# Layer 3 of a four-layer graph kernel: carrying a neighbour count between blocks by a row of the mask instead of by a second matrix product

## The chip, the cores and the metric

The kernel runs on one core of a Trainium2 chip. The metric is the device time of one execution in microseconds (us). Three executions of the kernel before took 552.76, 553.60 and 554.91 us; the median is 553.6 us. The profile shows one execution of the same program on the same kind of core.

The engines are named as in the profile: PE is the matrix engine (PEld its weight loads), DVE the vector engine, ACT the scalar engine, POOL the GpSimd engine, and SP an engine that here only issues DMAs.

## The reference

The input is a feature matrix x of 3327 nodes by 64 features and an adjacency matrix adj of 3327 by 3327 floats, of which a small share is not zero. Four layers follow each other; each computes x = layernorm(x + layer(x)). Layer 0 reduces to a layer norm of x. Layer 1 is a hyperbolic attention that reads all of adj. Layers 2 and 3 are the ones that matter here:

```python
# layer 2: two hops
for k in range(2):
    agg = adj @ x
    x = tanh(concat([agg, x]) @ W[k])
# layer 3
support = input @ weight
mask = (adj != 0)
rank = cumsum(mask, axis=1)
deg = rank[:, -1:]
k = minimum(deg, 100.0)
pos = rank - (deg - k)
w = mask * where(pos > 0, 0.5 ** (k - pos), 0.0)
out = w @ support + bias
```

In layer 3 the weight of a neighbour j of node i is 0.5 to the power of the number of neighbours of i that come after j, and zero from the hundredth on. So each weight needs a count over all later columns of the row.

## The kernel before, in words

The host hands over adj transposed and padded to 3328 by 3328, so rows are neighbours j and columns are nodes i. Rows are cut into NB = 26 blocks of 128, one neighbour per partition. Columns are cut into two halves (HALF = 1664), each into CPH = 4 chunks of CW = 416. One block is 1664 KB in f32, half of one 832 KB. Seven blocks stay in SBUF through layer 2 (`kept`: 25 to 22, EARLY, which stay through layer 3 too, and 19 to 21, LATE); the others are loaded by SP each time they are used, into a ring of UNDER_WAY = 4 block buffers (`strm`, tile `at_l` in the profile) and MORE = 2 further ones (`more`, tile `bt_l`).

Instructions are issued in the order in which the program writes them on PE, ACT and DVE in layers 2 and 3 (manual schedules), and SP issues the block loads in program order, each as soon as its buffer is free.

**Layer 2** (`layers`, the loop over `order`): in each hop every block is multiplied in f32. `add(c, jb)` (line 421) makes one product of 64 output rows for either half of the columns, so a block is eight products, two of them side by side in the columns of the PE array; f32 products show as two records each. The last blocks (`end`) are done chunk by chunk in `chunk_end` (the tanh is line 506), before `top` and `bottom` (lines 373, 409, 412) prepare the next hop. Blocks still in their buffers at the end of hop 1 (`ready`) are used first in hop 2. DVE and ACT have little to do.

**Layer 3** walks over 52 steps q: for each half, block 25 down to block 0. For a step

- `masks` (line 341, DVE) turns the half block into a bf16 mask of zeros and ones. It reads a kept block or a tile `ah` which SP loads just before (line 339, four buffers). It is called for step q + AHEAD = q + 3, into a ring of AHEAD + 3 = 6 mask tiles.
- `count` (line 526, PE) multiplies the mask by a 128 by 128 matrix into the PSUM tile `cnt[c]`, c = 0 or 1, of two chunks each. `tri` has 100 * 128 on its diagonal and -128 for every later row, so the result is 128 * (100 - later neighbours within the block) where there is a neighbour and something not positive elsewhere.
- `read` turns `cnt[c]` into a weight: the maximum with zero as a 16-bit integer is the bit pattern of a bf16 power of two. ACT reads c = 0 (line 541), DVE reads c = 1 (line 539).
- `products` multiplies the weights, LEAD = 3 steps later, by the support, which is split in three bf16 parts: two of them in one product of 128 rows (`high`, line 722, four per step), and the third in 64 rows (line 737), of which GROUP = 9 steps' worth, 36 products, are done in one burst.

`advance(c, q)` carries the count from block to block in PSUM: after `cnt[c]` was read for step q, `count(c, rest, q)` adds the matrix `rest`, for which tri + rest is -128 everywhere, so that `cnt[c]` then holds -128 times the neighbours seen so far; then `count(c, tri, q + 1)` adds the next block. So PE makes eight count products per step, four with `rest` and four with `tri`. In each step PE's order is: high c = 0, advance c = 0, high c = 1, (burst,) advance c = 1.

The support itself (parts `s12` and `s3`) is finished during the first steps of layer 3, by a list of small pieces of work, `with_step`, of which one is done per step; `other_parts` (line 653) is where POOL takes part. When the first half is done (`turn`), its sums are taken out and normalised beside the second half's steps (`half_out`). In layers 2 and 3 POOL does nothing else, and no DMA is issued from POOL anywhere.

Of the kernel before, what the change touches and what calls it, by code (L numbers as in the profile page):

```python
# [10 lines left out]
F32 = mybir.dt.float32  # L11
BF16 = mybir.dt.bfloat16
# [7 lines left out]
P = 128  # L20
# [21 lines left out]
UNDER_WAY = 4  # L42
MORE = 2

# [32 lines left out]
def kernel(  # L77
# [73 lines left out]
    with nc.allow_non_contiguous_dma(reason="two short columns"):  # L151
# [30 lines left out]
        pattern=[[-1, P]], channel_multiplier=1,  # L182
    )

    center = both_m[:, :P]
# [21 lines left out]
    tri = const.tile([P, P], BF16, name="tri")  # L207
    rest = const.tile([P, P], BF16, name="rest")

# [88 lines left out]
    def layer_3_constants():  # L298
        nc.gpsimd.tensor_copy(tri, tri_f)
        nc.gpsimd.tensor_scalar(rest, tri_f, -1.0, -STEP, ALU.mult, ALU.add)  # L300

        nc.gpsimd.tensor_scalar(w3_dg, w3_dg, float(2**27), None, ALU.mult)
# [9 lines left out]
    def layers(ctx, x2, x3, begun_here, kept, ready, ahead_ctx, strm):  # L312

        cols = x2.rearrange("p n d -> p (n d)")

        more_ctx = ExitStack()
        more = more_ctx.enter_context(tc.tile_pool(name="more", bufs=MORE, reuse_waits="tile"))
        l3m = None
        in_order = ctx.enter_context(ExitStack())
        in_order.enter_context(tc.manual_schedule(engines={mybir.EngineType.PE}))  # L320
        steps = [(h, jb) for h in range(2) for jb in range(NB - 1, -1, -1)]
        mask, ws = {}, {}

        def masks(q):
            nonlocal l3m
            if l3m is None:
                more_ctx.close()
                l3m = ctx.enter_context(
                    tc.tile_pool(name="l3m", bufs=AHEAD + 3, reuse_waits="tile")
                )  # L330
            if q >= len(steps):
                return
# [8 lines left out]
            nc.vector.tensor_scalar(mask[q], at, 0.0, None, ALU.not_equal)  # L341

        groups = fours
# [50 lines left out]
        )  # L394
        with tc.tile_pool(name="l2p", bufs=2, space=PSUM, reuse_waits="tile") as l2p:
            for k in range(2):
# [86 lines left out]
                for i, jb in enumerate(order):  # L483
# [6 lines left out]
                    for c in range(CPH):  # L490
                        add(c, jb)
                    if k == 0 and begun_here:

                        if i == 8:
                            for c in range(CPH):
                                bottom(c)

                            warm_t = small.tile([P, 1], F32, tag="warm", name="warm_t")
                            nc.scalar.activation(warm_t, hT[:, :1], AF.Tanh)
                    if k and jb in held and len(held) == MORE:  # L500
                        for q in range(AHEAD + 3):
                            masks(q)
# [5 lines left out]
                if k:  # L508
                    break
                for c in range(CPH):  # L510
                    chunk_end(c)
# [10 lines left out]

        def count(c, mat, q, start):
            for e in range(2):
                of = slice((2 * c + e) * CW, (2 * c + e + 1) * CW)
                nc.tensor.matmul(  # L526
                    cnt[c][:, e, :], mat, mask[q][:, of], start=start,
                    stop=(mat is tri), skip_group_check=True,
                )
# [120 lines left out]
        def other_parts(i):  # L650
            sl = slots(i)
            nc.scalar.copy(s12[:, sl, 1, :], rr[:, sl])  # L652
            nc.gpsimd.tensor_tensor(s3[:, sl], rr[:, sl], s12[:, sl, 1, :], ALU.subtract)  # L653

        with tc.tile_pool(name="l3t", bufs=2, space=PSUM, reuse_waits="tile") as l3t:
# [15 lines left out]
            first_part(A)  # L671
            count(0, tri, 0, True)
            read(0, 0, False)
# [5 lines left out]
            finish(l3t, C)  # L679
            count(1, tri, 0, True)  # L680
            squares(C)
# [32 lines left out]
        def products(q, c):  # L714
# [12 lines left out]


            later.append((q, c))
            if not last:  # L730
                high(q, c)
            if last or c and len(later) == 2 * GROUP:
# [9 lines left out]
                if last:  # L742
                    high(q, c)

        def sums_out(h):
# [63 lines left out]
        def last_out(h, accT):  # L809
# [87 lines left out]
    with tc.tile_pool(name="l1", bufs=1) as l1:  # L897
# [462 lines left out]
        def near_end(mT, ljT, xm, sq_e, t_e, rows_63, x2):  # L1360
# [4 lines left out]
            with tc.tile_pool(name="l1e", bufs=1) as l1e, tc.tile_pool(  # L1365
# [242 lines left out]
                nc.gpsimd.tensor_copy(tri, tri_f)  # L1608
                nc.gpsimd.tensor_scalar(rest, tri_f, -1.0, -STEP, ALU.mult, ALU.add)

# [266 lines left out]
```

## Time and profile before

| What | Value |
|---|---|
| Median of the three runs | 553.6 us |
| Profiled execution: its own time, and its span | 552.76 us, 552.8 us |
| Layer 2, hops 1 and 2 | about 240 to 315 and 315 to 391 us |
| Layer 3: start, steps, end | 391 to 411, 411 to 539, 539 to 553 us |
| PE busy | 524.6 us, 95% of the span |
| DVE, ACT, POOL busy | 373.2, 275.2, 207.6 us |

The profile gives, for each group of instructions with the same line and shape, the number of them, the time for which at least one was under way, and the mean duration of one. Products on PE overlap, so the spacing of their starts, not the duration of one, is what a product costs. A bracket at the end of a line of the timeline tells how long the engine sat idle before it and what released it.

### The profile page before, as it was taken

What the parts mean: (1) busy time and instruction counts of PE and PEld (TensorE: products, weight loads), DVE (VectorE), ACT (ScalarE), POOL (GpSimd) and SP (SyncE); (2) the same over time, 40 slices, a digit from 0 to 9 for tenths busy, and PEclk for the clock granted to TensorE, in tenths of its full rate; (3) what the DMA queues carried; (4) which work ended last, traced back from release to release, by engine and by line L of the source; (5) the groups of instructions that cost most, each with busy time, mean ns of one, the idle gap of its engine ahead of it and who ended that gap; (6) DMA issues with size and microseconds to landing.
All of it is one profiled execution on the core that took longest, in us unless ns stands there. A gap on an engine that the chain in (4) does not pass through costs nothing.

```text
span 552.8 us, 7387 instructions
## 1 busy us (share of the span) xinstructions
PE 524.6 (95%) x2841; PEld 228.6 (41%) x2841; DVE 373.2 (68%) x553; ACT 275.2 (50%) x321; POOL 207.6 (38%) x85
## 2 busy tenths in 40 slices
PE   8879999999999999999999999999999999989991
PEld 5622222222222222854444444444455555645551
DVE  6789999999999999899000011200679769697733
ACT  4699999999999997620000100000365333433321
POOL 3599999999999999000000000000001000000000
PEclk9799999999999999899999999999999999999996
DMA  8979667666777626699999049999019994799601
GB/s 288 341 225 301 219 224 234 212 233 208 232 240 225 209 95 277 247 427 427 421 430 395 3 167 422 429 420 383 32 53 362 323 375 140 238 295 354 244 1 37
DMA packets 33892, 143.56 MB, mean 260 GB/s; under 512 B 10269, under 2 KB 11959, under 8 KB 28855
## 3 DMA queue, kind: packets, MB, share of 16 engines
q1 hardware_dynamic: 31511, 142.40, 69.9%
q10 hardware_dynamic: 2336, 0.59, 0.5%
q8 instruction: 24, 0.39, 0.3%
q14 instruction: 21, 0.17, 0.1%
HBM read 141.53 MB, written 0.87 MB: 258 GB/s over the span
## 4 chain that ended last, share of the span: by engine, by line
PE 66%; DVE 16%; ACT 11%; issue 5%; DVEq 0%; POOL 0%; ACTq 0%; POOLq 0%
PE cnt L421 26%; PE cnt L526 11%; DVE v L1124 8%; PE pq L1103 7%; PE acc L722 6%; ACT pq L1116 5%; ACT sg L1076 5%; PE acc L1133 4%; PE acc L737 3%; DVE a L1115 2%; DVE w L539 1%; DVE mask L341 1%; PE cnt L412 1%; PE idle L928 1%; PE pm L1416 1%
## 5 line engine op out<-in xcount | busy, mean ns | idle before, releaser
L1088 POOL TENSOR_TENSOR sg<-sg,at 128x1664 f32<-128x1664 f32 x44 | 163.9, 3751 | 2.0 <-ACT sg L1076 1.9
L1103 PE MATMUL pq<-riT,ljT 64*128 64x416 f32 x416 | 100.8, 561 | 10.3 <-DVE v L1124 6.2
L1116 ACT ACTIVATE pq<-pq,al,ga 128x832 f32<-128x832 f32 x104 | 104.7, 1011 | 11.0 <-DVE a L1115 11.0
L1124 DVE SCALAR_TENSOR_TENSOR v<-pq,a 128x832 f32<-128x832 f32 x104 | 105.4, 1014 | 3.6 <-ACT pq L1116 2.5
L1115 DVE SCALAR_TENSOR_TENSOR a<-pq,sg 128x832 f32<-128x832 f32 x104 | 105.2, 1012 | 0.5 <-PE prep_fours L1194 0.5
L1133 PE MATMUL acc<-v,xv 128*64 128x416 f32 x416 | 95.3, 537 | 0.0
L1076 ACT ACTIVATE sg<-lb,rb 128x1664 f32<-128x1664 f32 (+1 forms) x53 | 87.2, 1647 | 0.0
L541 ACT ACTIVATE w<-cnt 128x832 int16<-128x832 f32 x55 | 47.2, 862 | 71.2 <-PE cnt L526 71.1
L421 PE MATMUL cnt<-at_l,lj 128*64 128x416 f32 x448 | 80.3, 513 | 0.0
L653 POOL TENSOR_TENSOR s<-sq,s 128x384 bf16<-128x384 f32 (+1 forms) x4 | 4.1, 1024 | 197.9 <-ACT s L652 197.9
L506 ACT ACTIVATE x<-cnt 128x416 f32<-128x416 f32 x8 | 4.1, 517 | 130.6 <-PE cnt L421 130.6
L1103 PEld LDWEIGHTS pq<-riT,ljT 64*128 64x128 f32 x416 | 31.3, 184 | 83.7 <-DVE v L1124 82.8
L539 DVE TENSOR_SCALAR w<-cnt 128x832 int16<-128x832 f32 x49 | 50.1, 1022 | 21.2 <-PE cnt L526 20.8
L526 PE MATMUL cnt<-mask,rest 128*128 128x416 bf16 x200 | 51.5, 339 | 2.4 <-ACT w L541 1.4
L526 PE MATMUL cnt<-mask,tri 128*128 128x416 bf16 x208 | 53.5, 339 | 0.1
L722 PE MATMUL acc<-w,s 128*128 128x416 bf16 x208 | 52.5, 339 | 0.5 <-DVE hid L794 0.5
L421 PEld LDWEIGHTS cnt<-at_l,lj 128*64 128x64 f32 x448 | 31.9, 137 | 46.1 <-issue 45.2
L1133 PEld LDWEIGHTS acc<-v,xv 128*64 128x64 f32 x416 | 20.6, 134 | 61.7 <-issue 58.0
L341 DVE TENSOR_SCALAR mask<-ah 128x1664 bf16<-128x1664 f32 x42 | 43.5, 1035 | 1.0 <-DMA ah<-in_adjT 1.0
L409 DVE COPY lj<-pn_l 128x512 f32<-128x512 f32 (+1 forms) x4 | 2.4, 592 | 60.8 <-PE pn_l L373 60.8
L421 PE MATMUL cnt<-kept,lj 128*64 128x416 f32 x224 | 41.2, 513 | 0.0
L1088 POOL TENSOR_TENSOR sg<-sg,kept 128x1664 f32<-128x1664 f32 (+1 forms) x10 | 30.0, 3026 | 0.8 <-ACT sg L1076 0.8
(291 smaller groups left out, 413.8 us busy)
## 6 DMA issues: line engine op xcount, KB each, us to landing
at_l<-in_adjT SPq DMA_DIRECT2D x24, 1664.0 KB, 12.2
at<-in_adjT SPq DMA_DIRECT2D x44, 832.0 KB, 5.0
ah<-in_adjT SPq DMA_DIRECT2D x42, 832.0 KB, 6.5
bt_l<-in_adjT SPq DMA_DIRECT2D x8, 1664.0 KB, 16.7
kept<-in_adjT SPq DMA_DIRECT2D x7, 1664.0 KB, 9.2
lb<-lf_rows SPq DMA_DIRECT2D x2, 384.0 KB, 6.3
ljT<-ljT SPq DMA_DIRECT2D x4, 128.0 KB, 2.3
x<-in_x ACTq DMA_DIRECT2D x1, 416.0 KB, 5.4
```

The costliest lines, as they stand in the source:

```text
L341: nc.vector.tensor_scalar(mask[q], at, 0.0, None, ALU.not_equal)
L421: nc.tensor.matmul(acc[c][h * D : (h + 1) * D, :], hw[:, slot(jb), :], blocks[jb][:, o : o + CW], start=c not in begun, stop=last, skip_gr ...
L526: nc.tensor.matmul(cnt[c][:, e, :], mat, mask[q][:, of], start=start, stop=(mat is tri), skip_group_check=True,)
L539: nc.vector.tensor_scalar(w.bitcast(I16), cnt[c], 0.0, None, ALU.max)
L722: nc.tensor.matmul(acc[h, c][:, e, :], s12[:, slot(jb)].rearrange("p t d -> p (t d)"), ws[q, c][:, e, :], start=first, stop=last,)
L1076: nc.scalar.activation(sg[:, :, of], lbs[:, :, of], AF.Sigmoid, bias=rb[:, sl : sl + 1])
L1088: nc.gpsimd.tensor_tensor(sg[:, :, of], sg[:, :, of], at[:, :, of], ALU.mult)
L1103: nc.tensor.matmul(pq[:, h, :], ljT[h != jb // NBH][rows, of], riT[rows, ch * CW : (ch + 1) * CW], start=True, stop=True,)
L1115: stt(a_s[t], pqs[t], CUBIC_PLUS, us.pop(t), op0=ALU.add, op1=ALU.mult)
L1116: nc.scalar.activation(pqs[t], pqs[t], AF.Square, bias=al[:, one], scale=ga[:, one])
L1124: stt(w, pqs.pop(t), CUBIC_REST, a_s.pop(t), op0=ALU.add, op1=ALU.mult)
L1133: nc.tensor.matmul(accs[cp, ci][h * D : (h + 1) * D, :], xv[:, slot(jb), :], w[:, h, :], start=(jb == orders[cp][0]), stop=(jb == orders[c ...
```

## The change

Layer 3 no longer carries the count in PSUM. The number of neighbours in all later blocks is computed beforehand, in layer 2, and handed to layer 3 in row 0 of each mask:

- In layer 2, `t_masks` makes masks of every block on DVE (two halves per block, ring of three tiles), and `t_counts` multiplies them by a 128 by 32 matrix of ones and zeros (`upto`) into two PSUM tiles `t_0`, `t_1`: four products of 32 output rows per mask, one per chunk and per quarter of the array's columns. Row r of the result is the number of neighbours in blocks r and later. Blocks from position 6 of hop 1 on are done in hop 1, the rest of the kept blocks at its end, and blocks 0 to 4 in hop 2.
- When all 26 blocks are counted, `t_out` clamps the counts at 127, writes them to DRAM (`t_rows`, four DMAs from POOL); `first_weights` loads row 0 of each block (eight DMAs from POOL) and works out the weights of the 26 first nodes.
- `masks` gets a DMA from POOL that overwrites row 0 of each of the 52 masks by the row of counts of the later blocks. Row 0 of `tri` becomes -128 throughout, so the product with `tri` subtracts them. `rest` is gone, and `count` starts a new sum for each step: four count products per step instead of eight.
- The first node of each block has lost its place in the mask; the 26 of them are an extra block of 32 rows. `first_rows` gathers their support rows into `sf` by 16 DMAs from POOL, issued with the seventh entry of `with_step` (step 9), and `first_products` adds eight products of 32 input rows per half, at block 12.
- `read` of c = 1 goes to DVE only in odd steps, and to ACT in even ones.
- MORE is 1 instead of 2, so one block buffer fewer in layer 2, and POOL too issues in program order.

```diff
-MORE = 2
+MORE = 1
+CLAMP = 127.0
+FIRST_T = 6
...
+    nc.gpsimd.memset(tri_f[:1, :], -STEP)
...
+        tmask = more_ctx.enter_context(tc.tile_pool(name="tmask", bufs=3, reuse_waits="tile"))
         more = more_ctx.enter_context(tc.tile_pool(name="more", bufs=MORE, reuse_waits="tile"))
...
             nc.vector.tensor_scalar(mask[q], at, 0.0, None, ALU.not_equal)
 
+            nc.gpsimd.dma_start(mask[q][:1, :], t_rows[jb + 1 : jb + 2, half])
...
+        def t_masks(jb):
+
+            t_done.add(jb)
+            for h in range(2):
+                m = tmask.tile([P, HALF], BF16, tag="tm", name=f"tm_{jb}_{h}")
+                nc.vector.tensor_scalar(
+                    m, blocks[jb][:, h * HALF : (h + 1) * HALF], 0.0, None, ALU.not_equal
+                )
+                t_made.append((jb, h, m))
+
+        def t_counts():
+            while t_made:
+                jb, h, m = t_made.pop(0)
+                for c in range(CPH):
+                    nc.tensor.matmul(
+                        t_ps[h][c * 32 : (c + 1) * 32, :], upto[:, 31 - jb : 63 - jb],
+                        m[:, c * CW : (c + 1) * CW], start=(h, c) not in t_begun,
+                        stop=len(t_done) == NB, skip_group_check=True,
+                    )
+                    t_begun.add((h, c))
+
+        def t_out():
+
+            for h in range(2):
+                nc.vector.tensor_scalar(tb[:, h], t_ps[h], CLAMP, None, ALU.min)
+            for c in range(CPH):
+                nc.gpsimd.dma_start(
+                    by_chunk(t_rows)[c], tb[c * 32 : c * 32 + NB + 1]
+                )
+
+        def first_weights():
+
+            firsts = by_chunk(adjT.rearrange("(b p) i -> p b i", p=P)[0])
+            for h in range(2):
+                nc.gpsimd.memset(m0, 0.0)
+                for c in range(CPH):
+                    nc.gpsimd.dma_start(m0[c * 32 : c * 32 + NB, :], firsts[c, :, h])
...
                     for c in range(CPH):
                         add(c, jb)
+                    t_counts()
+                    if jb not in t_done and (k or i >= FIRST_T):
+                        t_masks(jb)
...
-                    if k and jb in held and len(held) == MORE:
+                    if k and len(t_done) == NB and not t_made and not mask:
+                        t_out()
+                        first_weights()
                         for q in range(AHEAD + 3):
                             masks(q)
...
+                for jb in kept:
+                    if jb not in t_done:
+                        t_masks(jb)
+                        t_counts()
                 for c in range(CPH):
                     chunk_end(c)
...
-            first = steps[q + 1][1] == NB - 1
-            if not first:
-                count(c, rest, q, False)
-            count(c, tri, q + 1, first)
+            count(c, q + 1)
...
+            if c and jb == NBH - 1:
+                first_products(h)
...
+        def first_rows():
+
+            with nc.allow_non_contiguous_dma(reason="one row of each block"):
+                for cg in range(CPH):
+                    e = cg % 2
+                    for h in range(2):
+                        at = slice(cg * 32 + h * NBH, cg * 32 + (h + 1) * NBH)
+                        nc.gpsimd.dma_start(
+                            sf[at, 0, :],
+                            s12[:1, h::2].rearrange("p n t d -> p n (t d)"),
+                        )
+                        nc.gpsimd.dma_start(sf[at, 1, e * D : (e + 1) * D], s3[:1, h::2])
+
+        def first_products(h):
+
+            for part in range(2):
+                for cg in range(CPH):
+                    of = slice(cg * 32, (cg + 1) * 32)
+                    nc.tensor.matmul(
+                        acc[h, cg // 2][:, cg % 2, :], sf[of, part], tb[of, h],
+                        start=False, stop=False,
+                    )
...
-            lambda: other_parts(E), lambda: x3_later(C), lambda: x3_later(E),
+            lambda: (other_parts(E), first_rows()), lambda: x3_later(C), lambda: x3_later(E),
...
-            read(1, q, True)
+            read(1, q, q % 2 == 1)
```

More of the change, by code (lines that the diff above doesn't have):

```diff
@@ L207 @@
     tri = const.tile([P, P], BF16, name="tri")
-    rest = const.tile([P, P], BF16, name="rest")
     def block(pool, jb, **kw):
@@ L299, in layer_3_constants @@
         nc.gpsimd.tensor_copy(tri, tri_f)
-        nc.gpsimd.tensor_scalar(rest, tri_f, -1.0, -STEP, ALU.mult, ALU.add)
         nc.gpsimd.tensor_scalar(w3_dg, w3_dg, float(2**27), None, ALU.mult)
@@ L314, in layers @@
         cols = x2.rearrange("p n d -> p (n d)")
+        carry = ctx.enter_context(tc.tile_pool(name="carry", bufs=1, reuse_waits="tile"))
+        upto = carry.tile([P, 64], BF16, name="upto")
+        nc.gpsimd.memset(upto[:, :32], 1.0)
+        nc.gpsimd.memset(upto[:, 32:], 0.0)
+        tb = carry.tile([P, 2, CW], BF16, name="tb")
+        m0 = carry.tile([P, CW], F32, name="m0")
+        sf = carry.tile([P, 2, P], BF16, name="sf")
+        nc.gpsimd.memset(sf, 0.0)
+        t_rows = dram.tile([NB + 1, NP], BF16, name="t_rows")
         more_ctx = ExitStack()
+        tmask = more_ctx.enter_context(tc.tile_pool(name="tmask", bufs=3, reuse_waits="tile"))
         more = more_ctx.enter_context(tc.tile_pool(name="more", bufs=MORE, reuse_waits="tile"))
@@ L319, in layers @@
         in_order = ctx.enter_context(ExitStack())
-        in_order.enter_context(tc.manual_schedule(engines={mybir.EngineType.PE}))
+        in_order.enter_context(
+            tc.manual_schedule(engines={mybir.EngineType.PE, mybir.EngineType.Pool})
+        )
         steps = [(h, jb) for h in range(2) for jb in range(NB - 1, -1, -1)]
@@ L394, in layers, with by_chunk @@
         )
-        with tc.tile_pool(name="l2p", bufs=2, space=PSUM, reuse_waits="tile") as l2p:
+        def by_chunk(rows):
+            return rows.rearrange("b (h c k) -> c b h k", h=2, c=CPH)
+        t_done, t_made, t_begun, t_ps = set(), [], set(), []
+        def t_masks(jb):
[29 more added lines that the diff above has]
+                    nc.gpsimd.dma_start(m0[c * 32 : c * 32 + NB, :], firsts[c, :, h])
+                nc.vector.tensor_scalar(
+                    m0, m0, 0.0, (NEIGH + 1) * STEP, ALU.not_equal, ALU.mult
+                )
+                nc.vector.scalar_tensor_tensor(
+                    m0, tb[:, h], -STEP, m0, op0=ALU.mult, op1=ALU.add
+                )
+                nc.vector.tensor_scalar(tb[:, h].bitcast(I16), m0, 0.0, None, ALU.max)
+        with tc.tile_pool(
+            name="l2p", bufs=2 if begun_here else 1, space=PSUM, reuse_waits="tile"
+        ) as l2p:
+            t_ps += [
+                l2p.tile([P, 512], F32, bufs=1, tag=f"t{h}", name=f"t_{h}")[:, :CW]
+                for h in range(2)
+            ]
             for k in range(2):
@@ L515, in layers, with count @@
                 hT = nxt
-        def count(c, mat, q, start):
+        def count(c, q):
             for e in range(2):
@@ L526, in count @@
                 nc.tensor.matmul(
-                    cnt[c][:, e, :], mat, mask[q][:, of], start=start,
-                    stop=(mat is tri), skip_group_check=True,
+                    cnt[c][:, e, :], tri, mask[q][:, of], start=True, stop=True,
+                    skip_group_check=True,
                 )
@@ L671, in layers @@
             first_part(A)
-            count(0, tri, 0, True)
+            count(0, 0)
             read(0, 0, False)
@@ L679, in layers @@
             finish(l3t, C)
-            count(1, tri, 0, True)
+            count(1, 0)
             squares(C)
@@ L743, in products @@
                     high(q, c)
+        def first_rows():
[7 more added lines that the diff above has]
+                            s12[:1, h::2].rearrange("p n t d -> p n (t d)"),
+                        )
+                        nc.gpsimd.dma_start(sf[at, 1, e * D : (e + 1) * D], s3[:1, h::2])
[6 more added lines that the diff above has]
+                        start=False, stop=False,
+                    )
         def sums_out(h):
@@ L1608, in near_end @@
                 nc.gpsimd.tensor_copy(tri, tri_f)
-                nc.gpsimd.tensor_scalar(rest, tri_f, -1.0, -STEP, ALU.mult, ALU.add)
         def any_norm(m, x1):
```

## The prediction

> **What bounds the kernel now.** I read the engines' shares first, then the busy time by stage, then the chain of waits, and last the timeline of single steps.
>
> ```profile
> PE 524.6 (95%) x2841; PEld 228.6 (41%) x2841; DVE 373.2 (68%) x553; ACT 275.2 (50%) x321; POOL 207.6 (38%) x85
> ...
> 240.00:315.00 75.00, 75.00 (x423) 30.80 (x418) 21.20 (x42) 1.75 (x4) 0.00 (x0) 1.00 0.85 358
> 315.00:391.00 76.00, 76.00 (x432) 32.48 (x429) 8.75 (x11) 1.28 (x3) 0.00 (x0) 1.00 0.82 337
> ...
> 411.00:468.00 57.00, 56.70 (x354) 31.00 (x351) 48.65 (x53) 22.02 (x28) 2.07 (x2) 1.00 0.81 300
> ...
> PE cnt L421 26%; PE cnt L526 11%; DVE v L1124 8%; PE pq L1103 7%; PE acc L722 6%; ACT pq L1116 5%; ACT sg L1076 5%; PE acc L1133 4%; PE acc L737 3%; DVE a L1115 2%; DVE w L539 1%; DVE mask L341 1%; PE cnt L412 1%; PE idle L928 1%; PE pm L1416 1%
> ```
>
> The stage lines read: stage, its length, busy time of PE, PEld, DVE, ACT, POOL, then clock, DMA share and GB/s. PE is busy for all 75.00 and 76.00 us of the two hops, so whatever is added to PE there is added to the end; DVE (21.20, 8.75) is nearly free there. In layer 3's steps PE is busy for 56.70 of 57.00 us. The chain agrees: its largest pieces are the adds of layer 2 (L421) and the counts of layer 3 (L526).
>
> One step of layer 3:
>
> ```profile
> 436.63 1.02 DVE L341 TENSOR_SCALAR mask<-ah 128x1664 bf16<-128x1664 f32 x1
> 436.81 0.86 ACT L541 ACTIVATE w<-cnt 128x832 int16<-128x832 f32 x1 [1.25 <-PE cnt L526]
> 436.90 0.52 PE L526 MATMUL cnt<-mask,rest 128*128 128x416 bf16 x2
> 437.25 0.51 PE L526 MATMUL cnt<-mask,tri 128*128 128x416 bf16 x2
> 437.60 0.52 PE L722 MATMUL acc<-w,s 128*128 128x416 bf16 x2
> 437.80 1.02 DVE L539 TENSOR_SCALAR w<-cnt 128x832 int16<-128x832 f32 x1 [0.15 <-PE cnt L526]
> ...
> 438.92 0.86 ACT L541 ACTIVATE w<-cnt 128x832 int16<-128x832 f32 x1 [1.25 <-PE cnt L526]
> ...
> 449.65 3.36 PE L737 MATMUL acc<-w,s 128*64 128x416 bf16 x36
> 452.94 0.52 PE L526 MATMUL cnt<-mask,rest 128*128 128x416 bf16 x2
> ```
>
> A step is 438.92 - 436.81 = 2.11 us: twelve products starting 0.176 us apart. Each ninth step has the burst: 36 products, two abreast, in 3.29 us (0.091 each), with the switch 3.38. Nine steps: 9 x 2.11 + 3.38 = 22.4 us, 2.49 a step; ACT waits 1.25 us per step for PE.
>
> **Part 1, narrow products in layer 2: +18.5.** 52 masks, four products each, 416 columns. Four abreast a mask costs one start, 0.176. If only two run abreast as in the burst, 4 x 0.091 = 0.364; one after the other, 4 x 0.176 = 0.70. The burst is nearest (also a part of the array's columns, own weight load each) and shows overlap; four quarters should overlap further, so I take the middle of the first two, 0.27: 14.0. The program's order has 22 separate groups of them between the f32 adds; two changes of product shape cost 0.2 (the burst takes 3.38 where 18 x 0.176 = 3.17 would do): 4.4. Sum 18.5; ends 13.6 and 41. It all lies on the path.
>
> **Part 2, masks of layer 2 on DVE: +4.7.** 104 halves at 1.02 (L341) would be 106; there are 52, 53 us, beside 151 us of PE with 30 us of DVE, so they are hidden, except at the end of hop 1. There, PE's order has 40 narrow products in a row: blocks 17, 18 and the kept 25, 21, 19. The ring of three masks lets DVE be three ahead, so it still has seven masks to make after the last add: 7 x 1.02 plus waits, about 8.1 us, while PE has ten masks' products, about 3.4, already counted. Nothing lies behind them in PE's order but `chunk_end`, which waits too. If DVE gets one mask further ahead, 3.7; no gain is possible. In hop 2 the counts are complete at about the eleventh of 26 blocks, 15 x 2.81 = 42 us ahead of layer 3, which covers `t_out`, `first_weights` (12 DMAs in turn) and the first six masks.
>
> **Part 3, one block buffer fewer: 0.** A load of 1664 KB takes 3.9 us at the 427 GB/s of the best slices; 15 loads are 58 us against 75 of PE, and PE gets slower. Hop 2 starts with five instead of six blocks; walking its order (five ready, five new, then three new to one kept) the tightest load lands some 4 us early. If one came late, 4 us.
>
> **Part 4, the steps of layer 3: -15.7.** PE's own work falls to 8 x 0.176 = 1.41 a step. Three other limits appear. (a) The loop through `cnt`: a read (ACT 0.86, DVE 1.02), 0.08 to the first count product, 0.58 from there to the next read (404.97 to 405.52 in the start of layer 3 shows 0.55; 436.20 to 436.81 shows 0.61). With ACT reading both tiles in even steps, starting at 0: c = 0 of the next step is ready at 1.52, ACT is free at 1.72, then c = 0 of the step after next is ready at 1.72 + 1.52 = 3.24. So two steps take at least 3.24, 1.62 a step, and with the burst 2.00. (b) DVE: two masks and a read, 3.06 in 3.24. (c) The row DMA. DVE's order ties mask q + 3 to the read of odd q. From the end of that read: mask 1.04, DMA L, one step 1.62, then 0.58 and DVE's read 1.02: four steps in 4.26 + L. L is the issue on POOL plus the landing. Nearest rows:
>
> ```profile
> ljT<-ljT SPq DMA_DIRECT2D x4, 128.0 KB, 2.3
> ...
> out<-hid SPq DMA_DIRECT2D x1, 64.0 KB, 3.4
> ...
> ljT<-ljT SPq DMA_DIRECT2D x2, 32.0 KB, 5.6
> ```
>
> SP takes 0.33 us to issue one (the `ah` DMA at 437.68). No DMA is issued from POOL before; I bound the issue by nearly nothing (0.05) and 1.1, a small POOL instruction (L653, 0.9 to 1.15), and take 0.6, a little under the middle of 0.33 and 0.9. For landing I take 2.9, between 2.3 and 3.4, since the row is one small row. L = 0.1 + 0.6 + 2.9 = 3.6, ends 2.4 and 6.7. In nine steps a loop of four with the burst takes 4 x 1.62 + 3.4 = 9.9, and the other five 5/4 x (4.26 + 3.6) = 9.8: 19.7, 2.19 a step against 2.49, over 49 steps 0.32 x 49 = 15.7. Ends: L = 2.4 gives 2.02, -23; L = 6.7 gives 2.74, +12. The loads of `ah`, 852 KB or 2.0 us at 425 GB/s, 42 in 52 steps, fit under 2.19.
>
> **Part 5, the sixteen first-row DMAs: +11.** They stand in POOL's queue behind `other_parts` at step 9 and ahead of the row of mask 12. At 2.1 a step they start about 2.9 us after step 9 begins (ACT's copy 0.6, POOL's 1.15 after the reads); mask 12's row is the seventeenth and lands 2.9 + 17 x 0.6 + 2.9 = 16 us after. PE wants it at step 11, at 2 x 2.1 + 0.9 = 5.1. PE stands for 11 us; DVE, ACT and `ah` are soon full and wait with it. Ends: nothing (issue 0.05), and 17 x 1.1 + 5.6 - 2.2 = 22.
>
> **Part 6, small edits: +1.2.** `first_products`, 2 x 8: abreast 0.7, one by one 2.8; I take 1.5, with its changes of shape. Between 402 and 409 PE waits for ACT three times (0.25, 0.20, 0.18) and loses two `rest` products in each round: -0.3. Half of DVE's reads leave the crowded turn (468 to 490): 0 to -2, I take 0.
>
> Sum on the profiled execution: 18.5 + 4.7 - 15.7 + 11 + 1.2 = +19.7, from 552.8 to 572.5. The median stands 0.8 above that execution: 573.
>
> **Two rules of the skill.** The trace shows POOL and DVE in each other's way: of the masks at 1.02, one took 1.70.
>
> ```profile
> 409.31 0.91 POOL L653 TENSOR_TENSOR s<-sq,s 128x384 bf16<-128x384 f32 x1 [8.62 <-ACT s L652]
> 409.40 1.70 DVE L341 TENSOR_SCALAR mask<-ah 128x1664 bf16<-128x1664 f32 x1
> ```
>
> If each row DMA's issue did this to a mask, DVE would need 2 x 1.70 + 1.02 = 4.42 in two steps, 2.21 a step: no worse than the 2.19 above. The Trainium skill, SBUF — State Buffer, section "SBUF: two separate sides", speaks against this change: the shared port is an exclusive lock, and a DMA issued from GpSimd cannot have its descriptors written while such a DVE instruction runs. By that rule a row waits up to one mask longer, L = 4.6, 2.33 a step, and part 4 brings 8, for 581 in all. The same skill's DMA: Bandwidth & Descriptors, section "Latency and other measured facts", gives about 1 us to the first byte for DMAs issued from GpSimd, against 0.6 for the others; with 1 us an issue part 5 is 18, and the sum 580. No run here shows either yet.
>
> **Rivals.** *POOL's DMAs cost next to nothing* (place: POOL's queue, parts 4 and 5; for it: POOL is idle in layer 3, and SP issues in 0.33; against it: none is in the trace). Then L = 2.4, part 4 brings 23 and part 5 nothing: 18.5 + 4.7 - 23 + 1.2 = +1.4, 555, not slower; with an issue over 0.1 us it already is, and only four abreast as well takes it to 550. *The rows land late*: L about 6, issue 1: part 4 turns to (9.9 + 5/4 x 10.3) / 9 = 2.53, +2, part 5 is 20: +46, 600; for it speaks the 5.6 of a 32 KB DMA beside block loads, and layer 3 has such loads all the time. *The narrow products run one by one*: part 1 is 41, 595; against it speaks the burst. *DVE becomes the bound* by the locking above: about the same time as forecast, 573.
>
> **How the numbers follow.** Forecast or the DVE case, 0.50; late rows 0.20; one by one 0.08; POOL nearly free 0.22, of which 0.13 ends below 550.8, 0.06 within half a per cent (which is what a measurement of this kernel can tell from no change) and 0.03 above. Faster 0.13, same 0.07 (with 0.01 from the forecast's lower edge), slower 0.80. The forecast's own range, from its ends one at a time, is 561 to 585. To leave out no more than 2 in 10 the range goes from 549 to 603.
>
> **What would show it.** Right: PE idle some 5 us between narrow products and the last adds of hop 1; hops about 23 us longer in all; no `rest`; steps near 2.2 us; one PE idle of about 11 us around the twelfth step, ended by a mask's DMA, with POOL's queue full of first-row DMAs. Wrong: narrow products at 0.044 us apiece and no idle PE at step 11 (then 550 to 555); PE idle for a mask's DMA in most steps (then near 600); a block load ending PE's waits in hop 2.

## The result, and the profile after

The changed kernel takes 613.4 us (median of 4 runs, 611.9 to 614.6) against 553.9 of the kernel before (median of 4 runs): a ratio of 1.107, 95% interval 1.104 to 1.110. The sign was forecast, the size was not: +19.7 us on the profiled execution was predicted, +58.2 was measured (span 611.0 against 552.8), and 613 lies above the range's upper end, 603. The profiled execution itself took 612.7, 0.7 under the median.

First the changed kernel's page: the engines' shares, the clock granted to PE in 40 slices of the span, and the by-line shares of the chain that ended last.

```profile
PE 527.8 (86%) x2865; PEld 211.2 (35%) x2865; DVE 404.9 (66%) x589; ACT 293.7 (48%) x345; POOL 254.2 (42%) x170
...
PEclk9999999999999999989997999999986877988897
...
PE cnt L495 17%; PE pq L1208 10%; PE acc L1238 8%; DMA mask<-t_rows 8%; PE cnt L609 4%; DMA at_l<-in_adjT 4%; DVE v L1229 4%; PE acc L802 4%; ACT pq L1221 3%; ACT sg L1181 3%; PE acc L819 3%; DVE mask L356 2%; PE t L432 2%; DVE xc L371 2%; DVE a L1220 1%
```

PE was busy for 95% of the span and is now busy for 86%, though its busy time is hardly changed (524.6 to 527.8). Two DMAs have come into the chain: the mask's row (`t_rows`, 8%) and layer 2's block loads (`at_l`, 4%). In the last ten slices of the clock row, which are layer 3, PE is granted 0.6 to 0.8 of full clock in eight.

By stage (columns as in the forecast's table: stage, its length, busy PE, PEld, DVE, ACT, POOL, clock, DMA share, GB/s); the stages are hop 1, hop 2, the start of layer 3, and the steps in two pieces:

```profile
238.00:336.00 98.00, 92.62 (x592) 33.41 (x588) 62.28 (x84) 1.75 (x4) 0.23 (x1) 0.95 0.68 275
336.00:420.00 84.00, 79.30 (x469) 32.13 (x467) 22.27 (x29) 1.03 (x2) 11.37 (x20) 1.00 0.80 319
420.00:440.00 20.00, 16.84 (x79) 8.90 (x80) 15.24 (x45) 12.80 (x22) 2.54 (x3) 1.00 0.13 55
440.00:472.00 32.00, 12.93 (x58) 5.63 (x57) 15.25 (x17) 10.43 (x15) 18.14 (x28) 0.78 0.80 269
472.00:598.00 126.00, 99.47 (x581) 48.09 (x578) 59.13 (x69) 54.15 (x66) 18.59 (x36) 0.88 0.55 195
```

Hop 1 runs from 237.66 to 336.06, 98.4 us where it took 75.9; hop 2 to 419.90, 83.8 where it took 75.3. From the first to the last `acc<-w,s` of layer 3 it is 162.1 us where it was 131.3; the row of the kernel before stands first:

```profile
L722 PE MATMUL acc<-w,s x208: 338/339/350, 407.1 to 538.4; 128*128 128x416 bf16 x104
```

```profile
L802 PE MATMUL acc<-w,s x208: 336/339/554, 436.2 to 598.3; 128*128 128x416 bf16 x104
```

So +22.5, +8.6 and +30.8; the rest, about -4, is spread over the start and end of the layers. PE is idle in both hops and above all in the steps, and its clock is 0.78 and 0.88 in the steps.

What PE waits for, from the groups of the changed kernel (busy time, mean ns of one, idle time before and what ended it):

```profile
L609 PE MATMUL cnt<-mask,tri 128*128 128x416 bf16 x208 | 61.2, 382 | 46.8 <-DMA mask<-t_rows 44.5 <-ACT w L624 1.7
...
L358 POOL DMA_DIRECT2D mask<-t_rows x52 | 28.4, 547 | 115.0 <-PE cnt L609 54.6 <-DVE mask L356 50.1 <-issue 8.0
```

The rows in its table of DMA issues (KB each, median us from issue to landing):

```profile
mask<-t_rows POOLq DMA_DIRECT2D x52, 3.2 KB, 4.6
```

44.5 of the 46.8 us that the counts of layer 3 wait are ended by a row's DMA. A row takes 0.547 us to issue and 4.6 us from there to land (median), though it is 3.2 KB.

One turn of the loop that the forecast called four steps, from the timeline:

```profile
506.96 1.02 DVE L622 TENSOR_SCALAR w<-cnt 128x832 int16<-128x832 f32 x1 [8.53 <-PE cnt L609]
...
507.90 1.95 DVE L356 TENSOR_SCALAR mask<-ah 128x1664 bf16<-128x1664 f32 x2
...
509.43 0.52 POOL L358 DMA_DIRECT2D mask<-t_rows  x1 [10.00 <-PE cnt L609]
...
510.12 1.02 DVE L622 TENSOR_SCALAR w<-cnt 128x832 int16<-128x832 f32 x1 [0.27 <-PE cnt L609]
510.37 0.49 POOL L358 DMA_DIRECT2D mask<-t_rows  x1 [0.42 <-PE cnt L609]
...
513.71 0.85 PE L609 MATMUL cnt<-mask,tri 128*128 128x416 bf16 x2 [3.34 <-DMA mask<-t_rows]
...
514.35 0.90 PE L802 MATMUL acc<-w,s 128*128 128x416 bf16 x2
...
515.05 0.90 PE L609 MATMUL cnt<-mask,tri 128*128 128x416 bf16 x2
...
518.83 1.02 DVE L622 TENSOR_SCALAR w<-cnt 128x832 int16<-128x832 f32 x1 [5.81 <-PE cnt L609]
```

DVE reads every second step, at 506.96, 510.12 and 518.83, so from the first to the third read is 11.87 us for four steps. The first of the two masks ends near 508.92, and PE counts it at 513.71: L, the time from a mask's end to its count, is 4.8. Of that, 0.5 passes before the issue, 0.5 in it and 3.8 from its end to the count. Behind that wait of 3.34 us the pairs of products start 0.64 to 0.70 apart, where 0.35 is usual: PE runs at half clock for over 5 us.

### The profile page after: what moved, and what is told of

Same layout as the page of the kernel before. It is cut to its first block, busy times and chain, and to the rows that moved or that the text cites. A ratio compares the mean times of both kernels' runs of the same rounds, so it can differ in the third digit from the quotient of the medians.

```text
span 611.0 us, 7776 instructions
## 1 busy us (share of the span) xinstructions
PE 527.8 (86%) x2865; PEld 211.2 (35%) x2865; DVE 404.9 (66%) x589; ACT 293.7 (48%) x345; POOL 254.2 (42%) x170
## 4 chain that ended last, share of the span: by engine, by line
PE 53%; DVE 17%; DMA 14%; ACT 8%; issue 5%; POOL 1%; DVEq 0%; POOLq 0%; ACTq 0%
PE cnt L495 17%; PE pq L1208 10%; PE acc L1238 8%; DMA mask<-t_rows 8%; PE cnt L609 4%; DMA at_l<-in_adjT 4%; DVE v L1229 4%; PE acc L802 4%; ACT pq L1221 3%; ACT sg L1181 3%; PE acc L819 3%; DVE mask L356 2%; PE t L432 2%; DVE xc L371 2%; DVE a L1220 1%
## 5 line engine op out<-in xcount | busy, mean ns | idle before, releaser
L624 ACT ACTIVATE w<-cnt 128x832 int16<-128x832 f32 x79 | 65.8, 863 | 87.1 <-PE cnt L609 86.8
L609 PE MATMUL cnt<-mask,tri 128*128 128x416 bf16 x208 | 61.2, 382 | 46.8 <-DMA mask<-t_rows 44.5
L495 PE MATMUL cnt<-at_l,lj 128*64 128x416 f32 x528 | 97.3, 516 | 4.7 <-DMA at_l<-in_adjT 4.7
L358 POOL DMA_DIRECT2D mask<-t_rows x52 | 28.4, 547 | 115.0 <-PE cnt L609 54.6
L622 DVE TENSOR_SCALAR w<-cnt 128x832 int16<-128x832 f32 x25 | 25.6, 1024 | 73.4 <-PE cnt L609 73.4
L802 PE MATMUL acc<-w,s 128*128 128x416 bf16 x208 | 59.8, 379 | 1.3 <-DVE hid L899 0.5
L495 PEld LDWEIGHTS cnt<-at_l,lj 128*64 128x64 f32 x528 | 36.1, 137 | 58.9 <-issue 50.3
L423 DVE TENSOR_SCALAR tm<-at_l 128x1664 bf16<-128x1664 f32 x32 | 31.8, 1024 | 29.2 <-PE t L432 26.5
L609 PEld LDWEIGHTS <-tri 128*128 128x128 bf16 x208 | 20.3, 106 | 75.5 <-issue 27.5
L495 PE MATMUL cnt<-kept,lj 128*64 128x416 f32 x224 | 44.6, 547 | 0.0
```

Source lines behind the costliest of these rows:

```text
L495: nc.tensor.matmul(acc[c][h * D : (h + 1) * D, :], hw[:, slot(jb), :], blocks[jb][:, o : o + CW], start=c not in begun, stop=last, skip_gr ...
L609: nc.tensor.matmul(cnt[c][:, e, :], tri, mask[q][:, of], start=True, stop=True, skip_group_check=True,)
L624: nc.scalar.activation(w.bitcast(I16), cnt[c], AF.Relu)
L802: nc.tensor.matmul(acc[h, c][:, e, :], s12[:, slot(jb)].rearrange("p t d -> p (t d)"), ws[q, c][:, e, :], start=first, stop=last,)
```

## The experiments

Differences to the changed kernel are taken between ratios to the kernel before (which ran beside each) and given in us by a kernel of 554; a step is counted from its first count to the next step's.

**Leaving the rows out (no_rows).**

```diff
-            nc.gpsimd.dma_start(mask[q][:1, :], t_rows[jb + 1 : jb + 2, half])
```

> Leaves out the DMA of a mask's row 0, so the carried count of later blocks is missing from the weights. Theory 'late rows': a step of layer 3 waits for the row's DMA (44.5 us of PE's idle time in 18 waits) and PE then runs at half clock. Without the DMA the steps fall from 3.09 us each (160.5 for 52) to the 2.0 of the forecast's loop through cnt with its burst, 104 us, and the 11.8 us stall at the eleventh step goes too: 45 to 55 us faster, near 563. Rival 'busy POOL and DVE': the steps are bound by masks, reads and the locking of the two; then DVE's 59 us in 126 should not allow it to be more than 15 us faster. Rival 'count loop': ACT and cnt bound the step, no more than the 11.8 us stall is gained.

565.6 us, ratio 1.0205 (1.0161 to 1.0248): 48 us faster. The stage of the steps is 116.7 us (437.1 to 553.8), 45.4 less, about as much as the 44.5 us of waits for rows. What PE's counts still wait for in this kernel (us in total, times, longest):

```profile
PE cnt L608 <- DVE w L621: 6.8, 8, 1.3
...
PE cnt L608 <- ACT w L623: 4.0, 9, 1.4
```

The late rows are the cost of layer 3; "busy POOL and DVE" and "count loop" fall. But the stage stays 12.7 above the 104 us that I expected without rows: DVE waits 15.3 us for `ah` loads here, so the loads do not quite fit under steps of that length.

**Making the rows earlier (ahead6).** Nine mask tiles instead of six, in two pools; `GROUP` gives up the space.

```diff
-GROUP = 9
+GROUP = 5
...
-AHEAD = 3
+AHEAD = 6
...
+            pool = l3m if q % (AHEAD + 3) < 7 else l3x
```

> Masks and their rows are made six steps ahead instead of three (nine mask tiles instead of six; for their space the burst comes each fifth step instead of each ninth, which costs 1 to 2 us). Theory 'late rows': the loop is then (4.26 + 4.8) us over seven steps, 1.3 us, below the 1.62 of the loop through cnt, so rows are no longer waited for in steady steps; the sixteen first-row DMAs still cost some 6 us: 36 to 48 us faster, 566 to 577. Rival 'POOL's or DVE's rate': each row needs POOL for 0.55 us and up to 1 us of waiting for the port, and distance doesn't help; within 12 us of the changed kernel.

575.4 us, ratio 1.0404 (1.0361 to 1.0447): 37 us faster. The stage is 123.0 us. A row takes as long as before, but PE waits for one only once, behind the sixteen first-row DMAs:

```profile
PE cnt L610 <- DMA mask<-t_rows: 7.4, 1, 7.4
PE cnt L610 <- DVE w L623: 6.4, 7, 1.8
```

```profile
mask<-t_rows POOLq DMA_DIRECT2D x52, 3.2 KB, 5.1
```

So POOL's rate is no limit: the distance of three steps against the time to landing is.

**Spreading the first-row DMAs (spread).** Two in each of steps 10 to 17, behind the mask's row; the products that use them go to block 4.

```diff
-            lambda: (other_parts(E), first_rows()), lambda: x3_later(C), lambda: x3_later(E),
+            lambda: other_parts(E), lambda: x3_later(C), lambda: x3_later(E),
...
+            if 10 <= q < 18:
+                first_rows(q - 10)
...
-            if c and jb == NBH - 1:
+            if c and jb == 4:
```

> The sixteen first-row DMAs go two at a time behind the row of a mask, in steps 10 to 17, and the products that need them move to block 4 of each half. Theory: POOL's queue of sixteen is what mask 12's row waited for; the 11.8 us stall goes, eight steps have up to 1.1 us more on POOL: 9 to 14 us faster, 600 to 604. Rival: the stall has another cause (landing beside block loads, DVE), then within 3 us of the changed kernel.

604.3 us, ratio 1.0897 (1.0861 to 1.0933): 9.6 faster, as expected. In the changed kernel the sixteen ended like this:

```profile
466.90 0.51 POOL L838 DMA_DIRECT2D sf<-s  x1
...
468.91 2.02 POOL L358 DMA_DIRECT2D mask<-t_rows  x4 [1.50 <-DMA sf<-s]
...
471.15 0.85 PE L609 MATMUL cnt<-mask,tri 128*128 128x416 bf16 x2 [11.78 <-DMA mask<-t_rows]
```

With two per step the longest wait for a row is 4.3 us.

**Why a row takes 4.6 us to land (no_ah).** The block loads of layer 3 are left out; its masks are all made of the four kept blocks.

```diff
-                at = l3w.tile([P, HALF], F32, tag="ah", bufs=4, name=f"ah_{h}_{jb}")
-                nc.sync.dma_start(at, adjT[jb * P : (jb + 1) * P, half])
+                at = kept[NB - 1 - q % EARLY][:, half]
```

> Leaves out the block loads of layer 3: all masks are made from the four kept blocks, so the weights are wrong; row DMAs, masks and counts stay. Theory 'the rows land late because of the block loads': the median from issue to landing falls from 4.6 to 2 to 3 us (a row issued with no load under way landed within 2), the loop of four steps from about 12 to 9 or 10 us: 20 to 30 us faster, 583 to 593; the 11.8 us stall at step 12 gets a little shorter. Rival 'the landing is POOL's own delay': 4 to 4.6 us stays, and the time within 6 us of the changed kernel.

579.7 us, ratio 1.0434 (1.0409 to 1.046): 35 us faster, more than the 20 to 30 expected. The same rows, with no block load beside them:

```profile
mask<-t_rows POOLq DMA_DIRECT2D x52, 3.2 KB, 1.8
```

```profile
498.43 1.95 DVE L355 TENSOR_SCALAR mask<-kept 128x1664 bf16<-128x1664 f32 x2
...
499.96 0.51 POOL L357 DMA_DIRECT2D mask<-t_rows  x1 [2.68 <-PE cnt L608]
...
501.84 0.51 PE L608 MATMUL cnt<-mask,tri 128*128 128x416 bf16 x2 [0.95 <-DMA mask<-t_rows]
```

The first of the two masks ends near 499.4, the count starts at 501.84: L is 2.4, half of the 4.8 beside loads. The changed kernel shows the same by itself: at 518 to 524 no block moves (DMA share 0.01), and the row issued at 521.30 is counted at 523.18, 2.4 us after its mask. PE's waits for rows fall to 19.6 us, of which 9.3 are the one behind the first-row DMAs; the others are mostly near 1 us, and the clock is full behind most of them, which may be why it is more than 20 to 30.

**Issuing the rows from ACT (act_rows).** One step later, behind ACT's reads.

```diff
-            nc.gpsimd.dma_start(mask[q][:1, :], t_rows[jb + 1 : jb + 2, half])
...
+                nc.scalar.dma_start(
+                    mask[q][:1, :], t_rows[jb + 1 : jb + 2, h * HALF : (h + 1) * HALF]
+                )
...
+            row(q + AHEAD - 1 if q > LEAD else -1)
             masks(q + AHEAD)
```

> The row's DMA is issued from ACT's queue, one step later than the mask is made, instead of from POOL's. It no longer waits for POOL's hold on the shared port (about 1 us after a mask) nor behind the sixteen first-row DMAs. Theory 'POOL's way of issuing is slow': the row lands in 2 to 3 us and the stall of 11.8 us goes: the steps go to about 2.0 to 2.2 us each, 30 to 45 us faster, 570 to 583. Rival 'the block loads in the 16 DMA engines make the row late, whoever issues it': landing stays at 4 to 5 us, and only the 11.8 us stall is gained, less up to 5 us for the later issue: 5 to 12 us faster. Rival 'ACT's queue is held up by the issue': slower than the changed kernel.

594.3 us, ratio 1.0727 (1.0674 to 1.0779): 19 faster, between the theories. The stage of the steps is 136.0 us, 26 less; waits for rows are 23.8 us in 19, the longest 2.9. But hop 2 became longer: by the profile a block load there waited for a row's DMA on SP's queue, a wait that the experiment itself brought in, and PE then waited 7.7 us for that load.

```profile
SPq L214 <- DMA mask<-t_rows: 18.3, 1, 18.3
```

Of the 26 us, 11.8 are the wait behind the first-row DMAs; so another queue alone, though the issue comes a step later, is worth some 14 more. The steps of the stage are still 19 us from those without rows. A row still arrives late from this queue:

```profile
484.59 0.22 ACTq L362 DMA_DIRECT2D mask<-t_rows  x1
...
489.02 0.51 PE L616 MATMUL cnt<-mask,tri 128*128 128x416 bf16 x2 [2.63 <-DMA mask<-t_rows]
```

The issue is shorter (0.22 us), but from its start to the count that waits for the row it is 4.4 us here, and 4.3 in the turn shown of the changed kernel. The landing beside loads stays, as the rival said; both the queue and the loads count.

**The half clock (warm and warm_at).** Both add products by a matrix of zeros; `warm` in each step, `warm_at` only where the changed kernel waited for a row.

```diff
+                if not first:
+                    for _ in range(2):
+                        nc.tensor.matmul(
+                            acc[h, c][:, 0, :], zero, ws[q, c][:, 0, :], start=False, stop=False,
+                        )
```

> Adds four products by a zero matrix to each step of layer 3 (two behind each tile's products), which add nothing to the sums; 0.70 us more on PE in each of 50 steps, 35 us of added work. Theory 'half clock': each wait of over 3 us for a row leaves PE at half clock, which makes four steps 11.9 us where (4.26 + 4.8) is 9.1; with less idle time the clock stays up and a step takes what PE needs, 2.11 and the burst, 2.5 instead of 3.0: 10 to 25 us faster although 35 us of work are added. Rival 'the clock is a by-product, the row's latency sets the steps': 0 to 5 us slower. Rival 'PE bound': 20 to 35 us slower.

625.2 us, ratio 1.1302 (1.1256 to 1.1349): 13 slower, a miss: the theory had it 10 to 25 faster. The stage is 174.5 us, 12.4 longer, for 33.8 us of added work. The steps between waits, which need 1.5 to 1.7 us, all became 2.11, so the fill mostly lay where nothing was to be filled. The next one tells more.

```diff
+FILL = {6: 10, 12: 50, 16: 10, 20: 10, 24: 10, 34: 8, 36: 10, 42: 10, 46: 10}
...
                     products(p, c)
+                    for _ in range(FILL.get(q + 1, 0) if c == 0 else 0):
+                        nc.tensor.matmul(
+                            acc[steps[p][0], 0][:, 0, :], zero, ws[p, 0][:, 0, :],
+                            start=False, stop=False,
+                        )
```

> Products by a zero matrix, which add nothing to the sums, stand only where PE waited for a row in the changed kernel: 8 or 10 of them (1.4 to 1.8 us) ahead of the counts of steps 6, 16, 20, 24, 34, 36, 42 and 46, whose waits were 2.1 to 4.0 us, and 50 (8.8 us) at step 12, whose wait was 11.8. They fill waits and should lengthen nothing else. Theory 'half clock lies on the path': after such a wait the next step takes 2.73 instead of 1.5 to 1.7 us and the burst 6.69 instead of 4.8; with waits of 1 to 2 us left the clock stays, each of the nine saves 1 to 2 us: 9 to 20 us faster, 594 to 604. Rival 'the slow step only fills the next wait': within 4 us of the changed kernel.

606.2 us, ratio 1.0948 (1.0896 to 1.1): 7 faster (give or take 3), between the theories. The stage from 472 on, to be read beside the last row of the stages above:

```profile
472.00:598.00 126.00, 102.69 (x664) 53.66 (x660) 63.80 (x83) 53.86 (x69) 18.62 (x36) 0.99 0.56 195
```

The clock goes from 0.88 to 0.99. The lengths of steps 16 to 19, from the starts of their counts (the last of the four holds the next wait; the row of `no_ah` is beside them):

```
            16     17     18     19    sum
after      2.73   3.43   1.67   5.15   12.98
warm_at    1.63   1.99   1.70   5.01   10.33
no_ah      1.52   1.97   1.70   2.67    7.86
```

So the half clock behind a wait lies on the path, here with 2.65 us in four steps; over the kernel it is 7 us, 5.1 of them in this stage by the trace. Part of the gain went into longer waits: what PE stood or was filled with is 28 + 23 us, against 45 before.

**Narrow products (few_counts).** All are left out but those of the first block; the masks are still made.

```diff
                 jb, h, m = t_made.pop(0)
+                if (h, CPH - 1) in t_begun:
+                    continue
...
-                        stop=len(t_done) == NB, skip_group_check=True,
+                        stop=True, skip_group_check=True,
```

> Leaves out the narrow products of all blocks but the first, so that the counts of later blocks are wrong; the masks are still made on DVE. Theory 'four abreast': eight narrow products cost 0.46 us and the change of shape 0.14; 25 blocks are 15 us on the path, and the wait for masks at the end of hop 1 goes with them (5 us and up to 3 of half clock): 15 to 24 us faster, 590 to 598. Rival 'one after the other': 200 products of 0.176 are 35 us, and it is 35 to 43 us faster. Rival 'the loads bound the hops by now': under 8 us.

594.5 us, ratio 1.0734 (1.0688 to 1.0781): 19 us faster. Hop 1 is 78.5 us (237.59 to 316.05) instead of 98.4; hop 2 is 82.2 (316.05 to 398.29), only 1.6 shorter: PE waits for block loads there instead.

```profile
PE cnt L497 <- DMA at_l<-in_adjT: 5.5, 7, 1.1
```

Four abreast holds, "one after the other" falls. In the changed kernel a block's adds with the eight narrow products behind them repeat every 3.41 us (270.66, 274.07, 277.48) and 16 adds alone are 2.81: 0.60 for eight products, 0.46 from the first of them to the next add and 0.14 more ahead of them. (200 products one after the other, at 0.176, would be 35 us.)

**The ends of hop 1 (l2_spread).** Three kept blocks' masks are made in mid-hop.

```diff
+                    if k == 0 and i in (9, 13, 17):
+                        t_masks([b for b in kept if b not in t_done and b not in order[i:]][0])
```

> Three of the kept blocks that are counted at the end of hop 1 are counted earlier, in the middle of hop 1. Theory: the end of hop 1 loses about 5 us because DVE makes masks while PE stands, and some 3 more because the adds that follow run at half clock; with three of five blocks gone from there, 4 to 8 us faster, 605 to 609. Rival: DVE's masks elsewhere in hop 1 are just as much in the way, then within 2 us.

607.0 us, ratio 1.096 (1.0919 to 1.1): 6 us faster, as expected. The wait that it shortens, in the changed kernel, and one that I had not seen:

```profile
261.44 0.36 PE L432 MATMUL t<-tm,upto 128*32 128x416 bf16 x4 [1.21 <-DVE tm L423]
...
262.28 0.36 PE L432 MATMUL t<-tm,upto 128*32 128x416 bf16 x4 [0.48 <-DVE tm L423]
...
262.57 4.71 PE L495 MATMUL cnt<-kept,lj 128*64 128x416 f32 x16
...
321.36 0.71 PE L432 MATMUL t<-tm,upto 128*32 128x416 bf16 x12
...
322.85 0.36 PE L432 MATMUL t<-tm,upto 128*32 128x416 bf16 x4 [0.78 <-DVE tm L423]
...
328.93 7.20 PE L495 MATMUL cnt<-kept,lj 128*64 128x416 f32 x32
```

From 321.36 to 328.93 PE and DVE take turns; the 32 adds after it take 7.20 us where 32 took 5.76 in the kernel before, so they begin at half clock, though each wait there is under 0.8 us. The same happens at 261, at the first masks of layer 2: DVE is busy with sixteen transposes until 260.2, PE waits, and its next 16 adds take 4.71 where 3.01 is usual.

**Late block loads in hop 2 (no_first_loads).** The eight loads for the first nodes are left out.

```diff
-                    nc.gpsimd.dma_start(m0[c * 32 : c * 32 + NB, :], firsts[c, :, h])
+                    pass
```

> Leaves out the eight DMAs that load row 0 of each block for the first nodes, so the first nodes' weights are wrong. In hop 2 the block loads' data rate is lower while POOL's queue moves small packets, and loads land after 11 to 16 us; PE waits for them 4.7 us. Theory 'POOL's small packets slow the loads': without them PE's waits for loads go, 4 to 6 us faster. Rival 'the buffers come free too late', because a block is held until its masks are made: within 2 us of the changed kernel.

605.8 us, ratio 1.0975 (1.0908 to 1.1042): 5 faster, give or take 4. In the trace hop 2 is 3 us shorter (336.37 to 417.18), and PE's waits for loads fall from 4.7 to 1.7 us. The rate goes with it; the same 26 us, in which both kernels still load blocks, changed kernel first (last column GB/s):

```profile
380.00:406.00 26.00, 22.27 (x128) 8.59 (x124) 1.73 (x4) 0.00 (x0) 5.45 (x11) 1.00 1.00 388
```

```profile
380.00:406.00 26.00, 24.90 (x143) 9.75 (x140) 8.32 (x12) 0.00 (x0) 5.23 (x10) 1.00 1.01 420
```

The DMA engines are busy throughout in both. With eight loads of 42 KB in small pieces from POOL's queue they move 388 GB/s, without them 420: 0.8 MB less in 26 us, 2 us of loading. "Buffers free too late" explains at most the 1.7 us left.

**All that helped (best).** `ahead6` and `spread`, three kept blocks in mid-hop, `FIRST_T = 7` (the first masks a block later, behind the transposes), and half of the first nodes' loads already in hop 1.

```diff
-FIRST_T = 6
+FIRST_T = 7
...
+                    if k == 0 and i in (9, 12, 15):
+                        t_masks([b for b in kept if b not in t_done and b not in order[i:]][0])
+                    if k == 0 and i == 14:
+                        first_weights((0,), True, True)
```

> All that helped, together: masks and rows six steps ahead (burst each fifth step), the first-row DMAs two at a time, counting of blocks in layer 2 one block later (away from the transposes on DVE) with the three kept blocks counted in mid-hop, and the first nodes' first row loads issued already in hop 1. Theory: from the 575 of 'six steps ahead', the wait of 7.4 us for a row goes, some 5 us at the end of hop 1, 3 to 5 at its early wait with the clock behind it, 1 to 2 of late loads in hop 2: 553 to 560, about the time of the kernel before, since the 15 us of narrow products stay. Rival 'the row DMAs still bind under the block loads': 563 or more.

558.8 us, ratio 1.0075 (1.0051 to 1.01): 55 us faster than the changed kernel, and still 4 slower than the kernel before. Its waits:

```profile
PE cnt L618 <- DVE w L631: 8.6, 11, 1.4
...
PE t L433 <- DVE tm L424: 2.3, 3, 0.8
PE cnt L499 <- DMA at_l<-in_adjT: 2.2, 2, 2.0
```

The steps of layer 3 take 115.9 us (427.1 to 543.0), 15.4 less than before the change: this is what the change brings there once rows are on time. It costs 20 in front of them, 427.1 against 407.1, of which 26 groups of narrow products at 0.60 are 15.6.

## Why the prediction was right and wrong

The direction was right; one part, the steps of layer 3, carries most of the miss.

*Part 1, narrow products, +18.5: right.* By the period 26 groups at 0.60 are 15.6; leaving them out gave 19, with the waits at the end of hop 1 in it. They run four abreast: at most 0.23 a mask (0.46 for two), between the bound of 0.176 and the 0.27 taken; the rest of the changes of shape is 0.14, not 0.2.

*Part 2, +4.7: right in place, short in size.* The wait at the end of hop 1 is there. Missing were the earlier wait at 261 behind the transposes (1.7 us) and the half clock behind both (1.7 us in the 16 adds there, 1.4 in the 32 at the end of hop 1).

*Part 3, 0: wrong.* The forecast's "if one came late, 4 us" is what happened: 4.7 us of waits for loads in hop 2. The walk through the loads was made at 427 GB/s and left out `first_weights`' own loads, which part 2 had counted as covered; with them the DMA engines moved 388 GB/s from 380 to 406, without them 420.

*Part 4, -15.7: the step that failed.* It should have been about +19 (30.8 less the 11.8 of part 5). The shape was right: a loop of four steps through the row's DMA, with waits at steps 16, 20, 24, 28, 32, 36 and 40 (and, later, at some in between). Its length was forecast as 4.26 + 3.6 = 7.86 and is 11.87 in the turn shown. Three terms:

- L is 4.8, not 3.6 (+1.2). The issue begins 0.5 us behind the mask's end, not 0.1, and from its end to the count is 3.8, not 2.9, because block loads run beside it; without loads L is 2.4. In other turns beside loads L is up to 6.1.
- From the awaited count to DVE's read I put 1.62 + 0.58 = 2.20; but that read waits for the second tile of the next step, one half step more. In the kernel without `ah` loads, at full clock, it is 2.9 (+0.7).
- In the turn shown it is 5.1, because PE ran at half clock (+2.2). The forecast put this term at nothing and gave no reason.

By the forecast's own sum, 11.87 in place of 7.86 gives (9.9 + 5/4 x 11.87) / 9 = 2.75 a step, +27 in 49 steps: most of the 34 by which layer 3 was missed (30.8 measured; -15.7 + 11 + 1.5 forecast). Turns differ, and the waits of steps 6 to 10 (7.2 us), where `other_parts` stands in POOL's queue too, are partly in these 49 steps, so the last 7 are not accounted for one by one. The clock's share is the least sure: one turn says more than half of the lengthening, the run with filled waits gave back 7 us. The floor was too low also: without any rows the steps bring 14.6, not the 24 that 2.00 a step would, and DVE waits 15.3 us for `ah` there. The sum itself has two slips: 2.49 less 2.19 is 0.30 a step, which makes part 4 -14.7 and the whole +20.7; and L = 6.7 gives 2.62 a step and +6, not 2.74 and +12. Neither explains the miss.

*Part 5, +11: right, in part by luck.* 11.8 us, at step 12, ended by a mask's DMA, with POOL's queue full; spreading gave 9.6 back. But the row was counted 18.3 us after step 9 began (452.86 to 471.15), not 16, since POOL spent 12.9 us on the sixteen (455.97 to 468.91), not 9.6; and PE wanted it at 6.5, not 5.1. The two errors mostly cancel.

*The rules.* The prediction let a row wait out the second mask, 1 us, by the Trainium skill, SBUF — State Buffer, section "SBUF: two separate sides": GpSimd cannot write a DMA's descriptors while such a DVE instruction holds the shared port. Three rows show such a wait, where a mask began close to the issue; one of them:

```profile
544.09 1.12 POOL L358 DMA_DIRECT2D mask<-t_rows  x1 [4.13 <-PE cnt L609]
544.09 1.02 DVE L356 TENSOR_SCALAR mask<-ah 128x1664 bf16<-128x1664 f32 x1
```

The issue takes 1.12 us instead of 0.5 and ends 0.1 us after the mask. In the usual turn it costs next to nothing: the issue of the first row of a pair ends 1.03 us after its mask (509.95 against 508.92), and that of the second, with no mask behind it, 1.00 (510.86 against 509.85). So the L of 4.6 by that rule came near the 4.8 measured by the wrong sum. The 1 us of DMA: Bandwidth & Descriptors is a time to the first byte, which I used as the length of an issue; an issue held POOL for 0.547 in the mean. What I left out, and should have weighed, is TensorE: Matmul & The Clock Gate, section "Part 1: The HAM clock gate (the "warmup" mystery)": after an idle window of about 3.4 us the array is at half clock. The traces agree for long waits: in the changed kernel each of the five waits of 3.3 us or more is followed by a slow step (2.73, or 6.69 with the burst). They are less plain for shorter ones: behind a wait of 2.55 the step took 2.73, behind one of 3.14 it took 1.52, and the series of waits under 0.8 us at the end of hop 1 was followed by slow adds. So 3.4 us is no sharp bound here.

*The rivals.* "The rows land late" named the mechanism, with L of 6 and 600 us; L was 4.8 to 6.1 in the turns beside loads, and what made it worse than the price was the clock and the time from count to read. "POOL nearly free", "one by one" and "DVE the bound" fell.

## What to carry to other kernels

A small DMA in a loop is priced by the loop, not by its bytes: find how many steps it is ahead, and set its landing *beside the loads that run then* (4.6 us) against that distance; here three more tiles were worth 37 us. A wait of over 3 us for PE can cost more than itself, since the products after it often run at half speed (shorter waits did it too in some places here); look at the clock row of the stage, and in a forecast add it wherever such waits are predicted. Small pieces moved from one queue are not free for the large loads on another, so a transfer that nobody waits for still has a price.

## What the runs showed of the hardware

- A row of 3.2 KB issued from POOL lands in 1.8 us with no load beside it and in 4.6 to 5.1 with 832 KB loads on SP's queue (medians of 52 in `no_ah`, the changed kernel and `ahead6`). Issued from ACT beside such loads, one was counted 4.4 us after the start of its issue.
- A row's issue on POOL begins 0.5 us after the end of its mask and takes 0.5; where a DVE mask began with it, it took 1.12 and ended 0.1 us after that mask.
- Eight loads in small pieces from POOL's queue, 42 KB each, lowered the rate of the DMA engines, beside SP's block loads, from 420 to 388 GB/s over 26 us.
- Products of 128 by 32 weights into four different parts of a bank: eight of 416 columns between two groups of f32 adds lengthen these by 0.60 us, changes of shape included (3.41 against 2.81).
- 34 us of added products cost 12 us of time, and about 23 us of them, put where PE waited, made the kernel 7 us faster.
